# Layer 2 of a four-layer model: its fill between attention units handed out by a running credit, and tile pools that wait for the users of their own tile

## The chip, the core and the metric

The kernel runs on one core of one Trainium2 chip. A core has a matrix engine (TensorE, "PE" in the profile, with its weight loads shown apart as "PEld"), a vector engine (VectorE, "DVE"), a scalar engine (ScalarE, "ACT") that evaluates functions such as exp, tanh and gelu from tables, a general engine (GpSimd, "POOL") and a queue that issues most of the transfers (SyncE, "SP"). Matmul results land in PSUM, which this kernel splits into eight banks of 128 partitions by 512 fp32 numbers; everything else lies in SBUF. The engines run side by side and are held together by semaphores. The metric is the device time of one execution in microseconds.

## What is computed

The input `x` holds 8 sequences of 512 tokens with 128 features (fp32). Four layers follow one another, each of the same outer form: `xn = layernorm(x)`, then `x = x + attn(xn) * silu(ffn(xn))`. The layers differ in what attn and ffn are. Layer 0 is a recurrence with a routed ffn, layer 1 a feature-map attention with chosen experts, layer 3 a state-space block with an attention as its ffn. The change rewrites layer 2, which is this, for each sequence:

```python
def attn(x):                                   # 16 heads of 8 features
    q, k, v = split(ln(x, g_attn, b_attn) @ qkv_w + qkv_b)
    a = softmax(causal(q @ k.T / sqrt(8))) @ v  # for each head
    a = a @ out_w + out_b
    x = x + a
    ctx, xs, vs = a, ln(x, g1, b1), 0
    for _ in range(8):                          # ITERS
        u = tanh(ctx @ w_ctx + xs @ w_x + b_inl)
        vs = vs + 0.1 * (u - xs - vs)
        xs = xs + 0.1 * vs
    x = x + xs
    h = gelu(ln(x, g2, b2) @ ff_w1 + ff_b1)     # 512 wide
    return x + h @ ff_w2 + ff_b2

def ffn(x):                                     # hidden width 512
    h = silu(x @ w1.T * w1_s) * (x @ w2.T * w2_s)
    h = gelu(h @ h1.T * h1_s)
    h = gelu(h @ h2.T * h2_s)
    return h @ w3.T * w3_s
```

The product `ctx @ w_ctx` is the same in all eight iterations.

## The kernel before

The whole model is one program. Layers follow one another in time; `layer0`, `layer1`, `layer2` and `layer3` open their pools (SBUF tiles, and PSUM banks through `banks`, L95), load their packed constants (`load_consts`, L124, the load at L126 on SP's queue) and then issue their work. A tile pool puts tiles into memory that earlier tiles have left; the framework adds the waits for that. In layer 1 and 2, the order of PE is the order in which the code issues its matmuls (`manual_schedule`); the other engines' order follows from the same program text.

Between layers 1 and 2 stands `combine` (L176): it loads the experts' sum in two blocks (L184), takes its silu on ACT (L188), multiplies on DVE (L189) and adds to `x` on POOL (L194). Layer 2's first layernorm (L1226, with the subtraction at L1232) reads `x`. Between layers 2 and 3 the loads of layer 3's constants (L126 again) are the first thing that SP issues for layer 3, and its first matmul that needs them is L1658.

Layer 2 works with features on partitions. Its banks are `pu` (two tiles of two banks each, scores), `pf` (one bank, sums over keys) and `pa` (three banks, everything else).

- `begin(b)` (L1298): layernorm of sequence b, two transposes to feature order, projections to q, k and v (L1328 to L1345). The four heads of a group lie in strips of 32 partitions.
- `ffn(b)` (L1350): four steps of w1 and w2 with tanh for silu (L1359 to L1364), then h1 and h2. Each of these two is one step of sixteen 512-wide matmuls (L1372) with four gelus (L1373). Then one step of sixteen 128-wide matmuls for w3 (L1379).
- `maxima(b, g, qt)` (L1392): scores of query block qt against all keys up to it, 128 to 512 wide, four heads in two pairs. The matmuls at L1390 go to both `pu` tiles, a bf16 mask is added at L1401, and DVE takes the row maxima at L1404 into `mpad`. `put_maxima(b, g)` (L1406) transposes `mpad` (L1411) and adds it to a spare row of q (L1412), so that the scores come out with their maximum already taken off.
- `weights(b, g, kc)` (L1414): scores of key block kc against the queries from it on, 512 to 128 wide, again at L1390 into both `pu` tiles, with exp on ACT (L1422) and the causal cut on POOL.
- `sums(b, g, kc)` (L1426): weights times values and ones into `pf` (L1435), issued LAG = 2 units later.
- `group(b, g)` (L1443): transpose, divide by the sum, and for the last group of a sequence the output projection and `ctx` (L1466, L1468).
- `rest(b)` (L1471): layernorm, eight iterations (the matmuls L1485 with w_ctx and L1486 with w_x into one bank, tanh at L1488, updates on DVE at L1490 to L1493), layernorm, ff_w1 with gelu (L1509, L1510), ff_w2 in one step of thirty-two 128-wide records (L1515), and the gate and the addition to `x` (L1523 to L1527).

`begin`, `ffn`, `group` and `rest` are generators: each `yield` ends a step. One unit is one (sequence, group of four heads, key block), so a sequence has 16 units and the layer 128. The loop in `layer2` (L1531) issues for each unit u: its weights, one step of `back` (group and rest), at the end of a group the next `put_maxima`, one step of `front` (begin and ffn of the next sequence), the maxima of unit u + 5, one more step of back or front in turn, and the sums of unit u − 2. So each slot takes one step, however long that step is: between nothing and sixteen 512-wide matmuls. The five maxima ahead of the loop and all of `ffn(0)` come before the first weights; what is left of `rest` for the last two sequences comes after the last sums.

Of the kernel before, what the change touches and what calls it, by code (L numbers as in the profile page):

```python
# [80 lines left out]
class Kern:  # L81
# [12 lines left out]
    @contextmanager  # L94
    def banks(self, name, **bufs):  # L95

        with self.tc.tile_pool(name=name, bufs=1, space=PSUM) as pool:
            old, self.ps = self.ps, (pool, bufs)
            yield
            self.ps = old  # L100
# [230 lines left out]
def layer0(k, x, A, at):  # L331
# [5 lines left out]
    with ExitStack() as ctx:  # L337
        ctx.enter_context(k.banks("l0p", pa=5, pf=3))
        pool = lambda name, bufs=1, **kw: ctx.enter_context(tc.tile_pool(name=name, bufs=bufs, **kw))
# [123 lines left out]
        with tc.tile_pool(name="l0a", bufs=2) as tp, tc.tile_pool(name="l0a1", bufs=1) as tp1:  # L463
# [335 lines left out]
def choose1(k, cn, xT, idx, gate):  # L799
# [5 lines left out]
    with tc.tile_pool(name="ch", bufs=1) as pool, tc.tile_pool(name="ch2", bufs=2) as pool2:  # L805
# [112 lines left out]
class Layer1:  # L918
# [6 lines left out]
    def __init__(self, k, cp, x, A, at):  # L925
# [20 lines left out]
        with tc.tile_pool(name="l1a", bufs=2) as tp, tc.tile_pool(name="l1a1", bufs=1) as tp1:  # L946
# [16 lines left out]
    def choice_and_experts(self):  # L963
# [5 lines left out]
        with k.tc.tile_pool(name="l1w", bufs=2) as wp, k.tc.tile_pool(name="l1e", bufs=2) as ep:  # L969
# [163 lines left out]
def layer1(k, x, A, at):  # L1133
    nc, tc = k.nc, k.tc
    with ExitStack() as ctx:
        ctx.enter_context(k.banks("l1p", pu=2, pf=1, pa=3))
        pool = lambda name, bufs=1: ctx.enter_context(tc.tile_pool(name=name, bufs=bufs))
        L = Layer1(k, pool("l1c"), x, A, at)
        work = ExitStack()
        L.pools(lambda name, bufs: work.enter_context(tc.tile_pool(name=name, bufs=bufs)))  # L1140
# [40 lines left out]
def pack2(i):  # L1181
# [10 lines left out]
    p.add("own", one)  # L1192
    bq, bk = (strips2(b[None, n * C : (n + 1) * C]).reshape(2, P).T for n in range(2))
# [4 lines left out]
    bk[16::32] = -1.0  # L1198
    p.add("bk", bk)
# [58 lines left out]
class Layer2(BySequence):  # L1258


    def __init__(self, k, ctx, x, A, at):
        self.k, self.x = k, x
        nc, tc = k.nc, k.tc
        pool = lambda name, bufs=1: ctx.enter_context(tc.tile_pool(name="l2" + name, bufs=bufs))
# [33 lines left out]
    def begin(self, b):  # L1298

        k, nc, cn, tp = self.k, self.k.nc, self.cn, self.tp  # L1300
# [13 lines left out]
        yield  # L1314
        q["xT"] = tp.tile([P, T], F32, name="xT2", bufs=1)
        k.to_features(xn, q["xT"], nt=JT)
        yield
# [4 lines left out]
        yield  # L1322
        q["qT"] = tp.tile([P, 4, T], F32, name="qT2")
        q["kT"] = tp.tile([P, 2, T], F32, name="kT2")
        for t in range(2):
# [13 lines left out]
            yield  # L1339
# [8 lines left out]
        yield  # L1348

    def ffn(self, b):  # L1350
# [5 lines left out]
        for o in range(4):  # L1356
# [8 lines left out]
            yield  # L1365
        for n in ("h1", "h2"):
            src, hA = hA, hid()
            for o in range(4):
                ps = k.pa()
                for i in range(4):  # L1370
                    c0 = i * FF2 + o * P
                    nc.tensor.matmul(ps, fn[n][:, c0 : c0 + P], src[:, i, :], start=(i == 0), stop=(i == 3))  # L1372
                nc.scalar.activation(hA[:, o, :], ps, AF.Gelu, scale=fn[n + "_s"][:, o : o + 1])  # L1373
            yield
        f = q["f"] = tp.tile([P, JT, C], F32, name="f2", bufs=3)
        ps = k.pa((P, JT, C))
        for j in range(JT):
            for i in range(4):
                nc.tensor.matmul(  # L1379
                    ps[:, j, :], hA[:, i, j * P : (j + 1) * P], fn["w3"][:, i * C : (i + 1) * C],  # L1380
                    start=(i == 0), stop=(i == 3),
                )
# [779 lines left out]
```

## Time and profile before

Three runs of the kernel before took 3638.57, 3640.07 and 3646.86 us.

| | us |
|---|---|
| median of the runs | 3640.07 |
| the profiled execution, its own time | 3631.03 |
| its span (first to last instruction) | 3629.3 |
| layer 0 in the span | 0 to 885 |
| layer 1 | 885 to 1458 |
| layer 2 | 1458.6 to 2628.3 |
| of it: begin(0), five maxima, ffn(0) | 1458.6 to 1538.7 |
| of it: the 128 units | 1538.7 to 2558.0 |
| of it: the end of rest after the last sums | 2558.0 to 2628.3 |
| layer 3 | 2628.3 to 3629.3 |

Over the span PE is busy 2764.3 us (76%) with 16390 matmul instructions, DVE 2336.2 us (64%), ACT 1642.4 us (45%) and POOL 745.4 us (21%); the mean granted clock of PE is 0.835 of full speed. These are shares over stages with different limits, so each stage has to be read by itself. A row of the profile names a line of the code, an engine, an operation, its output and inputs with their shapes, how often it ran, and what the engine waited for just before it. Here is what a row of that kind looks like (from the page's part on the costliest groups: busy us, mean ns of one, idle us of the engine before it and what ended most of that):

```profile
L1372 PE MATMUL pa<-hid,f 128*128 128x512 f32 x512 | 222.7, 593 | 0.0
L1404 DVE TENSOR_REDUCE mpad<-pu 128x2 f32<-128x256 f32 (+3 forms) x256 | 199.2, 819 | 168.1 <-PE pu L1401 168.1
```

An fp32 matmul shows as two records in the trace, so L1372's 512 records are 256 matmuls. The mean of 593 ns is of the modelled durations, which overlap; the distance from one start to the next is what PE's time is made of. The row of granted clock over 40 slices, of which each is 90.7 us, reads 7 to 9 tenths in layer 2.

### The profile page before, as it was taken

Reading aid. Unit: us, or ns where it says so; the run is one execution under the profiler, and the core shown is the slowest. Engines: PE = TensorE matmul, PEld = TensorE weight load, DVE = VectorE, ACT = ScalarE, POOL = GpSimd, SP = SyncE. Lnnn points to the kernel's source line nnn. Section 1 sums busy time; section 2 is a strip of 40 time slices with the busy share of each in tenths; the row PEclk is TensorE's granted clock in tenths of the full one; section 3 lists DMA queues with packets and bytes.
Section 4 is the critical chain, followed back from the end, with each engine's and each line's share of the span. In section 5 each row is a group of like instructions: output and inputs, shape, how many; then the busy total and the mean of one; then the engine's idle time right before and its main releaser. Section 6 shows DMA issues by size and latency. Waiting matters only on the chain.

```text
span 3629.3 us, 44988 instructions
## 1 busy us (share of the span) xinstructions
PE 2764.3 (76%) x16390; PEld 1479.4 (41%) x16390; DVE 2336.2 (64%) x6346; ACT 1642.4 (45%) x3207; POOL 745.4 (21%) x845
## 2 busy tenths in 40 slices
PE   6164656512998898799999999998678877778777
PEld 4143444401444454344444444444334444444444
DVE  7989898998583234334445445445478787777776
ACT  5163545512544455233333333333266666655655
POOL 0004050400125553201101101101112222222121
PEclk8585757555789899799899899899878898878989
DMA  4003030311002222100000000000000000000000
GB/s 120 2 2 72 1 81 1 72 49 34 1 2 47 39 42 29 56 1 1 1 1 1 1 1 1 1 1 1 6 15 1 4 4 4 1 3 4 1 4 7
DMA packets 67519, 64.53 MB, mean 18 GB/s; under 512 B 5344, under 2 KB 59616, under 8 KB 66784
## 3 DMA queue, kind: packets, MB, share of 16 engines
q1 hardware_dynamic: 39264, 42.75, 3.8%
q0 software_dynamic: 19712, 14.69, 3.1%
q10 hardware_dynamic: 8320, 4.19, 0.4%
q8 instruction: 129, 2.11, 0.2%
q14 instruction: 94, 0.77, 0.1%
HBM read 43.80 MB, written 17.83 MB: 17 GB/s over the span
## 4 chain that ended last, share of the span: by engine, by line
PE 35%; DVE 16%; ACT 7%; issue 2%; POOL 2%; DMA 0%; POOLq 0%; ACTq 0%; DVEq 0%; SPq 0%
PE pa L1372 6%; PE pu L1390 6%; DVE nm L1972 4%; ACT at L1973 3%; PE pu L1969 3%; PE pf L1954 2%; DVE mpad L1404 2%; PE pf L1435 2%; PE pa L1486 1%; PE pa L1485 1%; ACT at L1422 1%; PE pa L1878 1%; PE pa L1509 1%; PE pa L1359 1%; PE pa L1515 1%
## 5 line engine op out<-in xcount | busy, mean ns | idle before, releaser
L1973 ACT ACTIVATE at<-pu,nm 128x512 f32<-128x512 f32 x512 | 347.9, 688 | 174.3 <-DVE nm L1972 154.5
L1972 DVE TENSOR_REDUCE nm<-pu 128x1 f32<-128x512 f32 x512 | 327.4, 683 | 75.4 <-PE pu L1969 74.8
L199 POOL TENSOR_SCALAR_AFFINE_SELECT at<-at 128x512 f32<-128x512 f32 x184 | 123.6, 672 | 1000.2 <-ACT at L1422 851.7
L1404 DVE TENSOR_REDUCE mpad<-pu 128x2 f32<-128x256 f32 (+3 forms) x256 | 199.2, 819 | 168.1 <-PE pu L1401 168.1
L1422 ACT ACTIVATE at<-pu 128x1024 f32<-128x1024 f32 (+3 forms) x256 | 171.8, 702 | 283.5 <-PE pu L1390 283.2
L1078 ACT ACTIVATE at<-pu,rsqrt 128x1024 f32<-128x1024 f32 (+3 forms) x256 | 191.1, 793 | 191.0 <-PE pu L1073 161.2
L1372 PE MATMUL pa<-hid,f 128*128 128x512 f32 x512 | 222.7, 593 | 0.0
L1969 PE MATMUL pu<-qT,kT 32*128 32x512 f32 x1024 | 203.1, 731 | 2.4 <-ACT at L1973 2.3
L1390 PE MATMUL pu<-qT,kT 32*128 32x512 f32 (+3 forms) x1024 | 160.6, 514 | 56.4 <-DVE mpad L1404 41.8
L748 PE MATMUL pa<-ident,Y 128*128 128x128 f32 x32 | 7.9, 425 | 211.2 <-DVE Y L739 211.2
L1954 PE MATMUL pf<-at,va 128*32 128x512 f32 x1024 | 163.1, 715 | 0.4 <-POOL va L1947 0.4
L1390 PE MATMUL pu<-kT,qT 32*128 32x128 f32 (+3 forms) x1024 | 150.8, 565 | 14.7 <-ACT at L1422 10.5
L548 POOL DMA_INDIRECT xg<-xn_d,idx x48 | 55.1, 1147 | 499.5 <-PE pf L552 318.5
L1372 PEld LDWEIGHTS pa<-hid,f 128*128 128x128 f32 x512 | 96.6, 190 | 119.5 <-issue 118.9
L1493 DVE SCALAR_TENSOR_TENSOR X<-X,u 128x512 f32<-128x512 f32 x56 | 38.7, 691 | 156.7 <-ACT u L1488 156.7
L1073 PE MATMUL pu<-qT,kT 32*128 32x512 f32 (+3 forms) x1024 | 130.3, 513 | 4.9 <-ACT at L1078 3.9
L1016 POOL DMA_INDIRECT f_d<-ys,idx x64 | 105.0, 1640 | 140.0 <-DMA f_d<-ys,idx 85.2
L1947 POOL TENSOR_TENSOR va<-V,sm 128x32 f32<-128x32 f32 x128 | 36.7, 286 | 463.6 <-DVE sm L1946 384.0
L1390 PEld LDWEIGHTS pu<-qT,kT 32*128 32x128 f32 x1024 | 67.3, 196 | 154.4 <-DVE mpad L1404 114.3
L1373 ACT ACTIVATE hid<-pa,f 128x512 f32<-128x512 f32 x64 | 44.0, 688 | 172.5 <-PE pa L1372 172.5
L1083 DVE TENSOR_TENSOR at<-at,ceiling 128x512 f32<-128x512 f32 x72 | 50.0, 695 | 102.3 <-ACT at L1078 91.4
L700 DVE TENSOR_TENSOR Z<-Hs,KE 128x96 f32<-128x96 f32 x510 | 108.8, 253 | 0.9
(610 smaller groups left out, 6682.8 us busy)
## 6 DMA issues: line engine op xcount, KB each, us to landing
w<-in_w_dram SPq DMA_DIRECT2D x24, 512.0 KB, 3.7
f_d<-zeros ACTq DMA_DIRECT2D x8, 512.0 KB
xn_d<-xn SPq DMA_DIRECT2D x8, 512.0 KB, 5.0
w<-in_w_dram SPq DMA_DIRECT2D x16, 256.0 KB, 3.2
w<-in_w_dram SPq DMA_DIRECT2D x24, 128.0 KB
f<-in_f_dram SPq DMA_DIRECT2D x1, 2888.0 KB, 11.9
xn<-in_x_dram SPq DMA_DIRECT2D x4, 512.0 KB, 9.0
Gt<-in_x_dram SPq DMA_DIRECT2D x4, 512.0 KB
```

What stands on the lines that cost most here:

```text
L199: self.nc.gpsimd.affine_select(a, a if src is None else src, pattern, ALU.is_ge, 0.0, base=0, channel_multiplier=-1)
L700: nc.vector.tensor_tensor(z[:, 0:3, v, :], bc(prev[:, v, :], 1, 3), bc(KE[:, o + t, 0:3, :], 2, 4), ALU.mult)
L1073: nc.tensor.matmul(pu[:, n, 0:m], q["kT"][r, g // 2, kc * P : kc * P + P], q["qT"][r, g, kc * P :], start=True, stop=True,)
L1078: nc.scalar.activation(at_[:, i : i + 2, 0:m], pu[:, :, 0:m], AF.Square, bias=k.rsqrt2, scale=32.0**-0.5)
L1372: nc.tensor.matmul(ps, fn[n][:, c0 : c0 + P], src[:, i, :], start=(i == 0), stop=(i == 3))
L1390: self.k.nc.tensor.matmul(pu[:, n, 0:m], a[r, c0 : c0 + P], b[r, q0 : q0 + m], start=True, stop=stop)
L1404: nc.vector.tensor_reduce(top[:, i : i + 2, 16], pu[:, :, 0:m], AX.X, ALU.max)
L1422: nc.scalar.activation(at_[:, i : i + 2, 0:m], pu[:, :, 0:m], AF.Exp, scale=8.0**-0.5)
L1954: nc.tensor.matmul(po[i * 32 : i * 32 + 32, :], va[:, kc, c0 : c0 + 32], E[:, i, :], start=(kc == 0), stop=(kc == JT - 1))
L1969: nc.tensor.matmul(pu, q["kT"][r, kc * P : (kc + 1) * P], q["qT"][r, g, :], start=True, stop=True)
L1972: nc.vector.tensor_reduce(nm[:, w], pu, AX.X, ALU.max, negate=True)
L1973: nc.scalar.activation(E[:, n, :], pu, AF.Exp, bias=nm[:, w], accum_out=sm[:, w])
```

## The change

The change has two parts.

**Pools.** Every tile pool and every group of banks in all four layers is opened with `reuse_waits="tile"`: a new tile waits for the users of the tiles whose bytes it takes, and not for users of the old pool as a whole. Nothing else changes in layers 0, 1 and 3.

```diff
-        with self.tc.tile_pool(name=name, bufs=1, space=PSUM) as pool:
+        with self.tc.tile_pool(name=name, bufs=1, reuse_waits="tile", space=PSUM) as pool:
```

The same argument is added in layer 0 (its main pools and "l0a"), in the choice of experts ("ch", "ch2"), in layer 1 ("l1a", "l1w", "l1e" and its main and work pools), and in the pools of layers 2 and 3.

**Layer 2's order.** Steps now yield what they cost in passes of a 512-wide matmul, and the loop hands them out by a running credit. The long steps are cut: h1 and h2 into half-steps of two matmuls, w3 and ff_w2 into halves, ff_w1 into two. The gelus of h1 and h2 read a bank of their own (`ph`), for which `pa` gives one up.

```diff
-        ctx.enter_context(k.banks("l2p", pu=2, pf=1, pa=3))
+        ctx.enter_context(k.banks("l2p", pu=2, pf=1, pa=2, ph=1))
...
             for o in range(4):
-                ps = k.pa()
+                ps = k.psum("ph", (P, T))
                 for i in range(4):
+                    if i == 2:
+                        yield 2.0
                     c0 = i * FF2 + o * P
                     nc.tensor.matmul(ps, fn[n][:, c0 : c0 + P], src[:, i, :], start=(i == 0), stop=(i == 3))
                 nc.scalar.activation(hA[:, o, :], ps, AF.Gelu, scale=fn[n + "_s"][:, o : o + 1])
-            yield
+                yield 2.0
```

`w_ctx @ ctx` is computed once for a sequence, at the end of `group`, and copied to SBUF; each iteration of `rest` adds it on DVE:

```diff
+        ps = k.pa()
+        nc.tensor.matmul(ps, cn["w_ctx"], ctx, start=True, stop=True)
+        q["ctx"] = tp.tile([P, T], F32, name="cw2")
+        nc.scalar.copy(q["ctx"], ps)
+        yield 1.0
...
-            nc.tensor.matmul(ps, cn["w_ctx"], q["ctx"], start=True, stop=False)
-            nc.tensor.matmul(ps, cn["w_x"], now, start=False, stop=True)
+            nc.tensor.matmul(ps, cn["w_x"], now, start=True, stop=True)
             u = tp.tile([P, T], F32, name="u2")
-            nc.scalar.activation(u, ps, AF.Tanh, bias=cn["b_inl"], scale=0.01)
+            nc.vector.tensor_tensor(u, ps, q["ctx"], ALU.add)
+            nc.scalar.activation(u, u, AF.Tanh, bias=cn["b_inl"], scale=0.01)
```

The maxima of two groups go to two spare rows of one `mpad` and are put into q together, so the maxima run nine units ahead (AHEAD = PAIR + 1) and not five, and their order inside a group is turned by one, which sets the wide weights beside narrow maxima:

```diff
+            top = self.mpad[g // 2][:, qt, :].rearrange("p (i c) -> p i c", c=32)
+            nc.vector.tensor_reduce(top[:, i : i + 2, 16 + g % 2], pu[:, :, 0:m], AX.X, ALU.max)
+
+    def put_maxima(self, b, t):
+
+        k, nc, qT, put = self.k, self.k.nc, self.q[b]["qT"], self.cn["put"]
         ps = k.pa((P, JT, P))
+        for qt in range(JT):
+            nc.tensor.transpose(ps[:, qt, :], self.mpad[t][:, qt, :], k.ident)
+        top = ps.rearrange("p a b -> p (a b)")
+        for v in range(2):
+            to = qT[:, 2 * t + v, :]
+            nc.vector.scalar_tensor_tensor(to, top, put[:, v : v + 1], to, ALU.mult, ALU.add)
```

And the loop: two slots in each unit, one behind the weights and one behind the maxima. A slot takes at most one step of group or rest, and then steps of begin and ffn of the next sequence (`front`) as long as its credit lasts.

```diff
+        U = 4 * JT
+        PAIR = 2 * JT
+        AHEAD = PAIR + 1
+        def maxima(u):
+
+            b, g, n = units[u]
+            L.maxima(b, g, (n - 1) % JT)
+
+        first = L.ffn(0)
         for u in range(AHEAD):
+            maxima(u)
+            next(first, None)
...
+        def fill(u, second):
+
+
+            nonlocal credit
+            wide = 1.5 - u % JT
+            share = (2.4 + 0.6 * wide, 2.4 - 0.6 * wide)[second] if u >= U else 1.8
+            share += 0.3 - 0.6 * second
+            passes = next(groups, None)
+            if passes is None:
+                passes = 0.0 if second and u % 2 == 0 else next(rest, 0.0)
+            credit = min(credit, share) + share - passes
+            while credit > 0.0:
+                passes = next(front, None)
+                if passes is None:
+                    break
+                credit -= passes
+
         for u in range(len(units) + LAG):
             b, n = divmod(u, U)
             if u < len(units):
                 held[u] = L.weights(*units[u])
+                if u % PAIR == PAIR - 1 and u + 1 < len(units):
+                    L.put_maxima(units[u + 1][0], units[u + 1][1] // 2)
+            fill(u, False)
             if u + AHEAD < len(units):
+                maxima(u + AHEAD)
+            fill(u, True)
             if u >= LAG:
                 wb, g, kc = units[u - LAG]
                 L.sums(wb, g, kc, held.pop(u - LAG))
                 if kc == JT - 1:
+                    groups = chain(groups, L.group(wb, g))
                     if g == 3:
+                        rest = chain(rest, L.rest(wb))
+
+            if n == LAG - 1 and b + 1 < B:
+                front = chain(L.begin(b + 1), front, L.ffn(b + 1))
+        for _ in chain(groups, rest):
+            next(front, None)
```

The lines that this block takes the place of are the loop described above (L1531 on). `w3` and `ff_w2` follow the same pattern as h1 and h2, two blocks of 128 tokens at a time, each half with its own PSUM tile and its own DVE instruction.

## The prediction

> **What bounds the kernel.** I read the busy rows by stretch first, because shares over the span mix four layers. Columns: window, its length, busy us (and instructions) of PE, PE's weight loads, DVE, ACT, POOL, then granted PE clock, DMA share, GB/s. The rows are layer 2's body (first weights to last of them), its steady part, two neighbouring pieces of one sequence, one piece split by clock, and the tail.
>
> ```profile
> 1538.70:2558.00 1019.30, 950.16 (x5335) 443.59 (x5334) 468.70 (x743) 366.85 (x529) 130.34 (x170) 0.93 0.00 1
> 1708.00:2399.30 691.30, 648.93 (x3572) 306.75 (x3571) 326.50 (x526) 251.46 (x362) 91.55 (x115) 0.93 0.00 1
> 2039.00:2083.00 44.00, 38.49 (x241) 19.56 (x244) 22.82 (x42) 15.79 (x22) 10.95 (x12) 0.77 0.00 1
> 2083.00:2122.60 39.60, 38.11 (x230) 16.86 (x223) 26.61 (x42) 16.80 (x26) 4.17 (x6) 1.00 0.00 1
> 2069.70:2083.40 13.70, 12.08 (x60) 5.90 (x60) 7.04 (x14) 3.21 (x5) 4.53 (x5) 0.50 0.00 0
> 2558.00:2628.30 70.30, 46.73 (x170) 23.93 (x170) 24.81 (x41) 15.49 (x23) 6.68 (x7) 0.81 0.00 0
> ```
>
> In the body DVE works 46% and ACT 36%; PE is the bound at 93% busy. Equal counts (241 and 230) take 44.0 and 39.6 us, though the first piece holds the narrower matmuls; it is at clock 0.77. PE's timeline (start, length, instruction, count, idle before) shows why:
>
> ```profile
> 1984.20 13.90 PE L1372 MATMUL pa<-hid,f 128*128 128x512 f32 x32
> ...
> 2060.81 1.14 PE L1390 MATMUL pu<-qT,kT 32*128 32x512 f32 x8
> 2061.88 3.84 PE L1515 MATMUL pa<-c,hid 128*128 128x128 f32 x32
> 2065.65 0.71 PE L1390 MATMUL pu<-kT,qT 32*128 32x256 f32 x8
> ...
> 2068.56 1.72 PE L1390 MATMUL pu<-qT,kT 32*128 32x384 f32 x8 [1.29 <-DVE mpad L1404]
> 2070.44 2.39 PE L1390 MATMUL pu<-kT,qT 32*128 32x384 f32 x8 [0.17 <-ACT at L1422]
> ```
>
> A whole h-step (13.9 us of PE) goes between two units, and then there is none for tens of us, in which PE waits for the score banks `pu`: for the maxima on DVE or the exp on ACT. The waits of layer 2 give the sum (us, times, longest):
>
> ```profile
> PE pu L1390 <- DVE mpad L1404: 45.7, 73, 1.7
> PE pu L1390 <- ACT at L1422: 23.5, 46, 1.5
> ```
>
> So 69 us are plain stall. The slowed matmuls add more: 512-wide strip groups take 1.07 us there (2060.81 to 2061.88) and 2.1 us at half clock.
>
> **PE's floor.** Pitches at full clock from these starts: a 512-wide fp32 record 0.43 us ((1998.03−1984.20)/32; one matmul is two records, 0.86); a 128-wide one 0.118 (3.77/32); strip groups of eight 1.07/0.86/0.65/0.43 by width; sums 0.99/0.79/0.59/0.36; a mask group 0.23. Per sequence: 130 wide records 55.9, 136 narrow ones 16.0, weights 4×3.01=12.0, maxima 12.0, masks 16×0.23=3.7, sums 4×2.73=10.9: 110.5 us against a period of 138.3 (the first h-step of each sequence starts at 1846.4, 1984.4, 2122.9). Summed over the body's records: 802 of 1019.3 us, a ratio of 1.27. The packed pieces do better: 2083–2122.6 floor 33.8 (1.17), 1950–1984 29.7 (1.144), 2016–2039 20.2 (1.14), all at clock 1.00; 2039–2083 25.3 (1.74).
>
> **The evening (fill, half-steps, order of maxima).** It moves no work off PE; it spreads a sequence's 66 us of fill (begin, ffn, group, rest) over 32 slots, about 2 us (2.4 passes of 0.86 from the second sequence on) behind every weights and every maxima. A score bank then has a slot plus a narrow neighbour to come free: a pair's maxima take DVE 0.42 to 1.22, its exp 0.39 to 1.02 on ACT. I take 1.14, the ratio of the two packed pieces that mix all kinds. The ends: 1.10 (single-group starts, no switching cost left) and 1.27 (nothing evened).
>
> **Removed from PE.** Per sequence 7 of 8 w_ctx matmuls (7×0.86=6.0), over seven sequences in the body 42; put_maxima once for two groups: 16×4 transposes less, 7.6; four maxima moved to the prologue, 2.4. New body floor 802−52=750. ×1.14=855: **−164**, of which 52×1.27=66 would come without evening.
>
> **Added.** DVE: one 0.69 us add per recurrence iteration, 5.5 a sequence, 65 to 71 us of 116: hidden beside fill. Each iteration is one slot, and its chain (matmul 0.86, add, tanh, update at 0.69) takes 3.2 us of some 3.6 between slots; uncovered it is 56×0.69=39. ACT: the gelus of h1 and h2 now stand alone between exps, so table loads rise from 29 to 133 by the built order; L1373's go from 8 to 55 and L1422's from 14 to 66. Shown before:
>
> ```profile
> L1422 ACT ACT_TABLE_LOAD x14 | 18.0, 1283 | 12.7 <-PE pu L1390 12.7
> L1373 ACT ACT_TABLE_LOAD x8 | 10.3, 1283 | 0.1
> ...
> 2062.03 1.28 ACT L1422 ACT_TABLE_LOAD   x1 [1.21 <-PE pu L1390]
> 2063.33 1.94 ACT L1422 ACTIVATE at<-pu 128x1024 f32<-128x1024 f32 x2
> ```
>
> 104×1.283=133 us more on ACT: 50 to 68 us per sequence of 116 (58%), and an exp whose load comes first frees its banks 1.28 late. The Trainium skill, "ScalarE: Activation LUTs", § What ACT_TABLE_LOAD costs, adds 1.38 us of drain to each, 2.66 in all, and its advice to batch calls by table set speaks against this change. By it ACT gets 277 us, 86 us per sequence of 116, and loads would reach PE. Here the exp starts 0.02 us after its load ended, so no drain: I take 133 us, and put its part on PE at nothing beyond the 1.14 (bounds 0 and 133). The single `ph` bank keeps a next step out until its gelu is done (load 1.28+0.69+0.25); the other half-step comes a slot later, so 0 (bounds 0 and 64×0.7=45).
>
> A second rule: "TensorE: Matmul & The Clock Gate", § HAM oscillation, asks for no PE-idle gaps above about 3.4 us. The idle pieces here are 1.5 us at most, so by it the evening could not bring the clock back. Half clock fills about 20 us of each 138 (6.8 and 13.7 us around 2046 and 2070), worth 10 us a sequence, 75 in all: the body would gain 89, the median be 3551. The trace halves the clock just where these small gaps cluster, in each sequence, so I keep the 164.
>
> **Prologue** (begin(0), maxima, ffn(0), 80 us): nine maxima interleaved with ffn instead of five ahead; stalls go, `ph` adds a gelu wait: 0±5. **Tail:** rest(7) alone, its iteration is
>
> ```profile
> 2592.11 0.69 ACT L1488 ACTIVATE u<-pa,c 128x512 f32<-128x512 f32 x1 [1.94 <-PE pa L1486]
> 2592.83 0.69 DVE L1493 SCALAR_TENSOR_TENSOR X<-X,u 128x512 f32<-128x512 f32 x1 [1.14 <-ACT u L1488]
> 2593.58 1.12 PE L1486 MATMUL pa<-X,c 128*128 128x512 f32 x2 [0.65 <-DVE X L1493]
> ```
>
> 2.63 us, with w_ctx's matmul hidden beside ACT. The add stands on this chain: 8×(0.69+0.04)=+6; halves of ff_w2 give 1 back: **+5**.
>
> **Pool waits.** Instruction order in layers 0, 1 and 3 is the same. Layer 1 to 2:
>
> ```profile
> 1442.93 7.70 SPq L184 DMA_DIRECT2D cmb_f<-f_d  x4
> ...
> 1449.32 2.36 DVE L189 TENSOR_TENSOR cmb_sg<-cmb_sg,s 128x1024 f32<-128x1024 f32 x2 [2.27 <-ACT cmb_sg L188]
> 1463.06 1.29 DVE L1232 TENSOR_TENSOR xn<-x,s 128x512 f32<-128x512 f32 x2 [2.23 <-POOL x L194]
> ```
>
> The loads waited for a DVE multiply at 1442.5; now only for the last scatter (issued 1431.5). SP carries them alone then, so Silu no longer ends the wait: 2.3 us. L1232 waits for its own tile, not POOL's last add: **−5** (0 to −7). Layer 2 to 3:
>
> ```profile
> 2636.12 0.56 PE L1658 MATMUL pa<-meet,c 128*128 128x4 f32 x2 [7.88 <-DVE meet L1655]
> ```
>
> Layer 3's constants still wait for layer 2's last ff_w2 matmul, so both loads queued on SP come as late: 0. Layer 0 to 1: the first gather moves 1 us earlier beside a bound DVE: 0.
>
> **Sum:** −164−5+5+0=−164. Profiled 3631.03→3467; the median of the runs is 9.04 higher, so **3476**.
>
> **Rivals.**
> A, evened as worked, ratio 1.11–1.19: 832–893 us of body, own range 3453–3515. Chance 0.60.
> B, the stalls nearly vanish (1.10 and below): 825, 3446 and down to 3425. For it: nothing but DVE and ACT latency stood behind them. Against: no mixed piece is that tight. 0.11.
> C, banks still come late (a unit's slot can be four transposes, 0.5 us, and two `pa` banks replace three) and only the removed work counts: 1.20–1.27, 3519–3574. 0.13.
> D, slower: table loads on PE's path. Place: exp at L1422 behind a gelu; `weights` and `maxima` share two `pu` pairs, so a load ahead of exp holds PE. Price: 104×1.28=133 less the 66 of removed work: +67, 3707 (3851 with the page's drain). It decides when evening brings nothing and each load costs PE over 66/104=0.64 us; had evening its full worth, 164/104=1.58 would be needed, more than a load lasts. For it: stalls on exp are there already. Against: after a load of before PE had a filled slot. 0.14.
> E, it does not do what it says: pool waits are unmoved where SP's next load hangs on the last matmul, and order gains nothing: about 3640. 0.02.
>
> **Numbers.** 3476 is A's. The range 3430–3580 holds A, C and half of B; D and the rest of B are out. A measurement tells about 0.2% (7 us; the runs spread over 8) from no change: faster A+B+C less a sliver 0.83, same 0.03, slower 0.14.
>
> **What would show it.** Body near 855 us and 116 us per sequence; clock near 1.00 throughout it; L1390's two waits mostly gone; 133 loads of 1283 ns with no PE wait behind them; tail iterations of 3.36 us; L1232 at about 1458. Wrong if PE's waits on L1422 or on L1373 (`ph`) grow past 60 us, or the clock stays at 0.93.

## The result and the profile after

Nine runs of the changed kernel have a median of 3628.42 us (3620.68 to 3629.41), nine of the kernel before, made beside them, 3640.07 (3634.27 to 3646.86). The ratio is 0.9964 with a 95% interval of 0.9954 to 0.9974: 9 to 17 us faster, where 164 were forecast. The profiled execution has a span of 3627.4 us, 1.9 us less than that of the kernel before, whose profiled execution lies 9 us under its median. So the rows below tell where time moved, and the runs tell how much it came to.

The rows by stretch come first again. The body now begins where the first ffn ends and ends at the last sums matmul, points that every kernel below has (the prediction's body, 1538.7 to 2558.0, was cut a little differently). The first two rows are of the kernel before, body and tail:

```profile
1535.50:2574.20 1038.70, 964.72 (x5421) 451.91 (x5419) 473.07 (x749) 371.54 (x535) 132.62 (x172) 0.93 0.00 1
2574.20:2628.80 54.60, 34.43 (x114) 16.80 (x102) 22.23 (x37) 10.81 (x16) 4.75 (x5) 0.81 0.00 0
```

and these are of the changed kernel:

```profile
1534.80:2553.50 1018.70, 899.25 (x5204) 401.12 (x5205) 505.00 (x810) 504.92 (x646) 131.97 (x172) 0.94 0.00 1
2553.50:2619.60 66.10, 33.32 (x100) 13.82 (x92) 27.54 (x45) 11.53 (x17) 5.67 (x6) 0.64 0.00 0
```

PE is busy for 65 us less in the body, but the body is only 20 us shorter: PE's idle (length less busy) went up from 74 to 119 us, and its clock is 0.94 where a packed piece has 1.00. The pitch floor of the body's records fell from 813.7 to 758.8 us, so the ratio to the floor rose from 1.28 to 1.34. (The floor is the prediction's: for each matmul record its distance to the next at full clock.) The tail is 11.5 us longer, at clock 0.64 in place of 0.81. ACT's busy time in the body rose by 133 us.

The two long waits of PE in the body of the kernel before (us, times, longest), with 8 us of others beside them:

```profile
PE pu L1390 <- DVE mpad L1404: 41.8, 68, 1.7
PE pu L1390 <- ACT at L1422: 23.5, 46, 1.5
```

and the longest of the changed kernel's, 118 us in all:

```profile
PE pu L1404 <- ACT at L1440: 29.5, 36, 1.9
PE pu L1404 <- DVE mpad L1419: 20.2, 19, 3.0
PE pa L1337 <- DVE xa L172: 12.8, 4, 5.4
PE pa L1507 <- DVE X L1515: 9.4, 10, 2.8
PE ph L1385 <- ACT hid L1386: 7.6, 7, 1.8
PE pa L1467 <- ACT oT L120: 6.1, 10, 1.5
PE pa L1370 <- DVE u L1509: 6.1, 5, 1.7
PE pa L168 <- DVE hr L1240: 6.0, 4, 4.1
```

The wait for maxima on DVE is halved, which is what the evening was to do. The wait for exp is 6 us longer. And the rows below these two hardly existed before. Most are waits for the inputs of the fill itself: `xa`, X, oT, the layernorm's `hr`, 43 us with the shorter rows of that kind. The row of L1370 is another kind. L1370 is w2's matmul, which does not read `u`; it waits until the add at L1509 has read the `pa` bank that it writes to. With six shorter rows of things that the waiting matmul does not read, PE waits 17.6 us for one of the two `pa` banks. Before, with three banks, no row of this kind is in the body.

The loads in front of exp stand in this group of the page (busy us, mean ns of one, idle before and what ended it):

```profile
L1440 ACT ACT_TABLE_LOAD x66 | 84.7, 1283 | 89.8 <-PE pu L1404 88.8
```

There are 133 table loads in layer 2, as forecast, of 1283 ns. The last column is the one that matters: ACT was idle for 88.8 us before these 66, and what ended the idle time was PE's scores. So the load mostly does not start when the gelu is done and ACT has nothing to do; in 47 of the 66 cases it starts after ACT has waited for the scores. (18 follow directly on other work of ACT.) The timeline of the changed kernel shows one of the 47, and what it holds up on PE:

```profile
2057.26 0.71 PE L1404 MATMUL pu<-qT,kT 32*128 32x256 f32 x8
2058.05 1.28 ACT L1440 ACT_TABLE_LOAD   x1 [3.11 <-PE pu L1404]
2058.14 0.66 PE L1467 MATMUL pa<-ident,oT 128*128 128x128 f32 x4 [0.17 <-DVE oT L122]
...
2059.34 1.09 ACT L1440 ACTIVATE at<-pu 128x512 f32<-128x512 f32 x2
2059.99 2.14 PE L1404 MATMUL pu<-kT,qT 32*128 32x384 f32 x8 [1.19 <-ACT at L1440]
```

ACT had been idle for 3.11 us when the scores came at 2058.05. Exp could have started there; the load comes first, and exp starts at 2059.34, 0.01 us after its end. PE does the one short fill step of that slot and then stands idle for 1.19 us, nearly as long as the load.

### The profile page after: what moved, and what is told of

It is laid out like the page before. It is cut to its first block, busy times and chain, and to the rows that moved or that the text cites. A ratio compares the mean times of both kernels' runs of the same rounds, so it can differ in the third digit from the quotient of the medians.

```text
span 3627.4 us, 44779 instructions
## 1 busy us (share of the span) xinstructions
PE 2698.3 (74%) x16214; PEld 1423.2 (39%) x16214; DVE 2384.1 (66%) x6426; ACT 1776.3 (49%) x3319; POOL 744.9 (21%) x845
## 3 DMA queue, kind: packets, MB, share of 16 engines
q8 instruction: 127, 2.08, 0.2%
## 4 chain that ended last, share of the span: by engine, by line
PE 31%; DVE 15%; ACT 10%; issue 2%; POOL 1%; POOLq 0%; ACTq 0%; DVEq 0%
PE pu L1404 5%; PE ph L1385 5%; DVE nm L2025 4%; ACT at L2026 3%; PE pu L2022 3%; PE pf L2007 2%; PE pf L1453 2%; ACT at L1440 2%; ACT L1440 1%; PE pa L1507 1%; DVE mpad L1419 1%; PE pa L1931 1%; PE pu L1416 1%; PE pa L1910 1%; POOL rs L1755 1%
## 5 line engine op out<-in xcount | busy, mean ns | idle before, releaser
L1419 DVE TENSOR_REDUCE mpad<-pu 128x2 f32<-128x1024 f32 (+3 forms) x256 | 198.9, 818 | 149.8 <-PE pu L1416 149.7
L1385 PE MATMUL ph<-hid,f 128*128 128x512 f32 x512 | 255.6, 626 | 11.6 <-ACT hid L1386 11.5
L1404 PE MATMUL pu<-kT,qT 32*128 32x512 f32 (+3 forms) x1024 | 135.7, 502 | 30.3 <-ACT at L1440 29.5
L1404 PE MATMUL pu<-qT,kT 32*128 32x512 f32 (+3 forms) x1024 | 127.2, 493 | 20.7 <-DVE mpad L1419 20.2
L1385 PEld LDWEIGHTS ph<-hid,f 128*128 128x128 f32 x512 | 94.6, 199 | 113.8 <-issue 89.7
L1073 PE MATMUL pu<-qT,kT 32*128 32x512 f32 (+3 forms) x1024 | 131.0, 515 | 4.8 <-ACT at L1078 4.0
L1016 POOL DMA_INDIRECT f_d<-ys,idx x64 | 104.6, 1635 | 138.2 <-DMA f_d<-ys,idx 86.8
L1440 ACT ACT_TABLE_LOAD x66 | 84.7, 1283 | 89.8 <-PE pu L1404 88.8
L585 POOL DMA_INDIRECT f_d<-ys,idx x48 | 83.9, 1748 | 109.9 <-ACT ys L584 81.2
L1404 PEld LDWEIGHTS pu<-kT,qT 32*128 32x128 f32 x1024 | 56.9, 189 | 123.3 <-ACT at L1440 79.6
```

What stands on the lines that cost most here:

```text
L1073: nc.tensor.matmul(pu[:, n, 0:m], q["kT"][r, g // 2, kc * P : kc * P + P], q["qT"][r, g, kc * P :], start=True, stop=True,)
L1404: self.k.nc.tensor.matmul(pu[:, n, 0:m], a[r, c0 : c0 + P], b[r, q0 : q0 + m], start=True, stop=stop)
L1419: nc.vector.tensor_reduce(top[:, i : i + 2, 16 + g % 2], pu[:, :, 0:m], AX.X, ALU.max)
L1440: nc.scalar.activation(at_[:, i : i + 2, 0:m], pu[:, :, 0:m], AF.Exp, scale=8.0**-0.5)
```

## The experiments

Each was run beside the kernel before; the ratio is to it. Names that begin with b are edits of the kernel before, those with a of the changed kernel. The table puts layer 2's body side by side (us; idle is length less PE busy; all from one profile each).

| kernel | body | PE busy | idle | PEclk | tail | ratio of times, interval |
|---|---|---|---|---|---|---|
| before | 1038.7 | 964.7 | 74 | 0.93 | 54.6 | 1 |
| b_hoist | 1053.0 | 929.2 | 124 | 0.93 | 68.0 | 1.0068 [1.0046, 1.0090] |
| changed | 1018.7 | 899.3 | 119 | 0.94 | 66.1 | 0.9964 [0.9954, 0.9974] |
| a_nohoist | 1053.0 | 933.2 | 120 | 0.94 | 55.1 | 1.0020 [1.0003, 1.0037] |
| a_tanh | 948.0 | 862.9 | 85 | 0.96 | 67.8 | 0.9778 [0.9757, 0.9800] |
| a_tanh_nohoist | 983.8 | 902.6 | 81 | 0.95 | 54.0 | 0.9844 [0.9825, 0.9862] |
| a_tanh_loose | 925.7 | 857.5 | 68 | 0.97 | 50.4 | 0.9662 [0.9635, 0.9690] |
| a_pre | 994.7 | 884.7 | 110 | 0.95 | 69.3 | 0.9906 [0.9886, 0.9927] |

**The loads taken away: a_tanh.** It computes tanh where the layer has gelu, and so needs no second table.

```diff
-                nc.scalar.activation(hA[:, o, :], ps, AF.Gelu, scale=fn[n + "_s"][:, o : o + 1])
+                nc.scalar.activation(hA[:, o, :], ps, AF.Tanh, scale=fn[n + "_s"][:, o : o + 1])
...
-            nc.scalar.activation(hid[:, o, :], ps, AF.Gelu, bias=cn["ff_b1"][:, o : o + 1])
+            nc.scalar.activation(hid[:, o, :], ps, AF.Tanh, bias=cn["ff_b1"][:, o : o + 1])
```

> The changed kernel with layer 2's gelus (h1, h2 and ff_w1) computed as tanh, so that exp and all of layer 2's functions come from one table and its 133 table loads fall away; instructions, shapes and order otherwise the same. Theory L (the extra table loads, 133 us of ACT, delay exp, gelu and tanh, and PE waits for them): PE's 118 us of idle in the body fall below 50, and the time goes from 3628 to about 3500 (3470 to 3540). Rival S (steps of the fill that depend on one another stand only one slot apart, and the latency of DVE and ACT without any load is already longer than a slot): the idle stays above 90 us, the time above 3595.

Measured: 0.9778, 3551.8 us. Against the changed kernel's 0.9964 that is 1.9% or 68 us, and its body is 71 us shorter. Over the 104 added loads that is 0.65 us each (0.68 by the body; the 29 old ones cost nothing, as the next run shows). PE's order is the same; its idle fell by 34 us and its busy time by 36, as the clock rose from 0.94 to 0.96. In the body of a_tanh the two kinds of wait on score banks read

```profile
PE pu L1404 <- DVE mpad L1419: 18.9, 20, 3.0
...
PE pu L1404 <- ACT at L1440: 2.8, 4, 1.1
```

so the wait for exp was made of loads (29.5 to 2.8 us), and the wait for maxima was not. Theory L holds for this part, but 85 us of idle are no matter of loads, and both the idle and the time lie between the two theories. Of the waits left, 21.7 us are for score banks, 17.9 for `pa` banks and 42 for inputs of the fill.

**The same in the order before: b_tanh.** The same two lines in the kernel before.

> The kernel before with the same three gelus as tanh: 29 table loads (37 us of ACT) fall away. Theory L: they stand mostly behind whole h-steps with ACT idle, so at most 20 us: 3620 to 3640. Rival S: 3635 to 3640. It is also the base for the run with tanh of the changed kernel: the gain of the new order without loads is the difference of the two.

Measured: 1.0012 [1.0005, 1.0019]: nothing gained. The 29 loads of the old order cost nothing. The likely reason is that PE had a long step beside them, as the ff_w2 step of 3.84 us beside the load at 2062.03 in the prediction's lines. (In both tanh kernels the order of a few DVE and ACT instructions in layer 3 shifts as well; its length there, 1012 and 1006 us, lies within the 1000 to 1012 that it has in all the profiles.)

**The pools alone: b_pools.** The `reuse_waits` argument on every pool and bank of the kernel before, no other edit.

> The kernel before with the pools' argument alone (every tile pool and bank waits by tile). Theory P1: it brings only the earlier combine between layers 1 and 2, 3 to 5 us: 3635 to 3637. Rival P2: it makes the whole measured difference of 12 us, and the new order of layer 2 brings nothing: 3626 to 3630.

Measured: 1.0005 [0.9996, 1.0015], no difference. Its profile shows the table load of layer 2's first exp at 1526.1 us where it was 1533.0, so the earlier entry is there; the body behind it was 9 us longer in that execution (clock 0.92). P2 is out: the 12 us are not the pools'. That the entry's gain reaches the end is not shown.

**w_ctx: a_nohoist, b_hoist, a_tanh_nohoist.** The first and the last put the matmul back into each iteration of the changed kernel, b_hoist takes it out of the kernel before (there with plain `yield`s). Each of these edits also takes away or adds the step of `group` in which the single matmul stands:

```diff
-            nc.tensor.matmul(ps, cn["w_x"], now, start=True, stop=True)
+            nc.tensor.matmul(ps, cn["w_ctx"], q["ctx"], start=True, stop=False)
+            nc.tensor.matmul(ps, cn["w_x"], now, start=False, stop=True)
             u = tp.tile([P, T], F32, name="u2")
-            nc.vector.tensor_tensor(u, ps, q["ctx"], ALU.add)
-            nc.scalar.activation(u, u, AF.Tanh, bias=cn["b_inl"], scale=0.01)
+            nc.scalar.activation(u, ps, AF.Tanh, bias=cn["b_inl"], scale=0.01)
```

> The changed kernel with w_ctx put back into each iteration (two matmuls, tanh straight from PSUM, no add on DVE). Theory H1 (PE's time is what counts, so the 42 us of matmuls taken off come back whole, times 1.1): 3660 to 3675, the tail 6 us shorter. Rival H2 (the chain of an iteration is what PE waits for, and the add on DVE made it 0.73 us longer 64 times): 3615 to 3640.

> The kernel before with w_ctx computed once in a sequence and added on DVE, nothing else: 56 matmuls of 0.86 us less, 49 us of PE. H1 (PE's time counts): 35 to 60 us faster. H2 (the longer chain takes a part back, as in the new order, where it was worth 20 to 24): 15 to 25 us faster, the tail 6 longer.

> The changed kernel with layer 2's gelus as tanh (no loads) and w_ctx back in each iteration: the evened order without loads and without the removed matmuls. Against the same kernel with w_ctx once, H1 (PE's time counts): 42 us and more slower, about 3597 where that took 3552. H2 (the longer chain of an iteration takes the gain back): within 20 us of it. Against the kernel before with tanh (3635) it gives what evening alone is worth: by the prediction's ratio 1.14 some 100 us, by what the runs have shown so far 30 to 50.

Measured: in the changed order the single w_ctx is worth 0.56% (1.0020 to 0.9964, 20 us), without loads 0.66% (24 us): 34 to 36 us in the body less 11 to 14 in the tail, between H1 and H2. But this is not w_ctx alone. Without its step, all of `rest` comes one slot earlier, and one slot in four takes no step of `rest`. In the changed kernel such a slot lies between the second layernorm of `rest` and the transposes that read it; in a_nohoist and a_tanh_nohoist the two are in neighbouring slots. (The kernel before has an empty step behind each layernorm of `rest`, which the new order drops.) PE's wait for `hr`, 6.0 us in the changed kernel and 7.4 in a_tanh, is in these two

```profile
PE pa L168 <- DVE hr L1240: 35.9, 7, 6.2
PE pa L168 <- DVE hr L1240: 33.4, 7, 5.0
```

so 30 and 26 us of the 34 and 36 may belong to where a step fell, and not to the matmul. No run separates them.

In the old order the single w_ctx costs 0.7%, 25 us (14 in the body, 13 in the tail), which neither theory had. PE is busy for 35 us less in the body and idle for 50 more. PE's waits in b_hoist's body:

```profile
PE pu L1390 <- DVE mpad L1404: 59.8, 65, 4.0
PE pu L1390 <- ACT at L1422: 19.2, 36, 1.5
PE pa L1490 <- DVE X L1498: 13.2, 15, 1.9
PE pa L1503 <- DVE X L1498: 9.0, 7, 2.6
PE pa L1514 <- ACT hid L1515: 7.9, 6, 1.3
```

The wait for the maxima is 18 us longer, and of the last three rows only the first was there before, with 0.5 us. A reading that fits, but was not tried by itself: DVE has 56 more adds in its queue, and where an iteration is the only fill of a slot, half its matmul time covers half as much.

From a_tanh_nohoist against b_tanh (0.9844 to 1.0012) the evened order with the pools is worth 1.7%, 61 us, with w_ctx in place and no loads (30 to 50 were expected), and this in spite of the 33.4 us of waiting for `hr`. With loads it is worth nothing: a_nohoist is 7 us slower than the kernel before. Step by step the measured change is +4 us from the kernel before to b_tanh, −61 to a_tanh_nohoist, +64 for the loads to a_nohoist and −20 to the changed kernel: −13. How the −61 and the −20 divide between the order and w_ctx stays open because of the wait for `hr`.

**The place of the load: a_pre, a_pre_m, a_m.** A one-column exp behind the gelus draws the load to where ACT is free:

```diff
                 nc.scalar.activation(hA[:, o, :], ps, AF.Gelu, scale=fn[n + "_s"][:, o : o + 1])
-                yield 2.0
+                b and nc.scalar.activation(self.warm, hA[:, o, 0:1], AF.Exp, scale=0.0); yield 2.0
```

and the same behind each pair of ff_w1's gelus. The scheduler still orders ACT by itself and puts the small exp behind a waiting one in a fourth of the cases, so a_pre_m holds ACT to program order; a_m does only that.

> The changed kernel with a one-column exp behind every gelu of layer 2 (not in the first ffn), and ACT held in program order there: there are 13 table loads more than in the changed kernel (146), but the load back to exp's table starts as soon as the gelu is done, not when the next scores have arrived on PE. Theory L1 (what hurts is the load's place, between the arrival of the scores and exp): PE's waits on exp fall from 29 us to under 10, the time by 30 to 60 us. Rival L2 (what hurts is the sum of the loads on ACT, wherever they stand): no gain, or slower by up to 15 us.

> The changed kernel with ACT held in program order in layer 2 and nothing else: the control for the run with the early load. All theories: within 10 us of the changed kernel, about 0.996 of the kernel before.

> The changed kernel with a one-column exp behind every gelu of layer 2 (not in the first ffn), ACT's order left to the scheduler as in the changed kernel: 146 loads, of which 54 of the 73 back to exp start with the gelu's end. Theory L1 (place of the load): with ACT held in order the same edit brought 0.7%; here 15 to 30 us faster than the changed kernel, 0.988 to 0.992 of the kernel before. Rival L2 (sum of the loads): 13 loads more, 0 to 10 us slower, 0.997 to 0.999.

Measured: a_pre_m 1.0011 [1.0000, 1.0022] against a_m 1.0080 [1.0063, 1.0096], 25 us faster with 13 loads more, a little under L1's 30 to 60. PE's wait for exp fell from 34.0 to 12.2 us, but that for oT, which ACT copies, rose from 9.2 to 27.7. a_m as a control missed: program order on ACT alone is 1.2% slower than the changed kernel, with 28.6 us of waiting for begin's layernorm that are not there in the changed kernel. a_pre is 0.9906, 21 us faster than the changed kernel. Its loads:

```profile
L1386 ACT ACT_TABLE_LOAD x57 | 73.1, 1283 | 1.0
L1387 ACT ACT_TABLE_LOAD x39 | 50.0, 1283 | 0.7
L1440 ACT ACT_TABLE_LOAD x19 | 24.4, 1283 | 9.7 <-PE pu L1404 9.2
```

L1387 is the small exp. These 39 loads back to exp's table start with hardly any idle before them (0.7 us in all), and only 19 loads still stand in front of an exp of scores. PE's wait for exp fell from 29.5 to 18.0 us. ACT's sum of loads went up by 17 us and the time down by 21: the load's place counts (L1), though not for all of the 68.

**Fewer loads: a_pair_m, a_g4, a_g4_gap.** a_pair_m gives `ph` two banks and `pa` one, and issues two gelus together. a_g4 scales on DVE and has one gelu for all four hidden blocks; a_g4_gap also lets the next slot go without a front step:

```diff
-                nc.scalar.activation(hA[:, o, :], ps, AF.Gelu, scale=fn[n + "_s"][:, o : o + 1])
-                yield 2.0
+                nc.vector.tensor_scalar(hA[:, o, :], ps, fn[n + "_s"][:, o : o + 1], None, ALU.mult)
+                if o == 3:
+                    nc.scalar.activation(hA, hA, AF.Gelu)
+                yield 2.0 if o < 3 else 4.4
```

(a_g4 has a plain `yield 2.0` there.)

> The changed kernel with two `ph` banks and one `pa`, the gelus of h1 and h2 in pairs, ACT in program order in layer 2: 83 loads and not 133. Theory L2 (sum of the loads): 50 loads of 1.28 us less, up to 38 us faster by the share that all 133 cost (66 of 170 us). Theory L1: as many exps with a load ahead as there are gelu pairs, 25 fewer, 15 to 30 us faster. Rival: the lone `pa` bank costs more than that, no gain or slower.

> The changed kernel with h1's and h2's scale applied on DVE (0.69 us each, which frees the `ph` bank), and one gelu over all four hidden blocks when the last is there: 57 table loads and not 133. Theory L (loads): 76 of the 104 added loads go, worth some 50 us by what all were worth (68): 0.982 to 0.987 of the kernel before. Rival S (dependent steps too close): h2's first matmul and w3's now wait for a gelu of 2 us and its load, some 4 us twice in a sequence, 60 us in all: no gain, 0.995 to 1.005.

> The same, and the step with the gelu counts 2.4 passes more, so that the next slot takes no front step, while each slot's share is 0.15 higher. Theory S: the wait for the gelu is covered by the units' own work, 15 to 40 us faster than without the gap. Theory L alone: the same within 8 us.

Measured: a_pair_m 1.0261 [1.0238, 1.0283], 66 us slower than its control a_m: the lone `pa` bank costs far more than 50 loads bring. (Wq's matmul alone waits 17.6 us there until kT's copy has read the bank, 2.3 in the control.) a_g4 0.9950 [0.9937, 0.9963], the same as the changed kernel although 76 loads are gone; rival S. With the gap 0.9904 [0.9883, 0.9925], 17 us faster than without, as S said. In a_g4 the wait for exp is 10 us shorter than in the changed kernel, but h2's and w3's matmuls wait 16.6 us for the single gelu. With the gap these 16.6 us are gone; the wait for `xa` fell as well (12.8 to 1.9) and that for exp rose (19.8 to 27.9), since the gap moves every later step of the fill. So distance behind a gelu helps, but the 17 us are not its own alone.

**The fill's own chains: a_tanh_loose.** On a_tanh, two dependences taken away by other data:

```diff
-            nc.tensor.matmul(ps, cn["w_x"], now, start=True, stop=True)
+            nc.tensor.matmul(ps, cn["w_x"], q["xT0"], start=True, stop=True)
...
-            nc.tensor.matmul(ps, cn["Wk"][:, ts], xa, start=True, stop=True)
+            nc.tensor.matmul(ps, cn["Wk"][:, ts], q["xT"], start=True, stop=True)
```

> The changed kernel without loads (gelus of layer 2 as tanh), and with two dependences of the fill taken away by other data: w_x's matmul of each iteration reads the ctx product and not the newest X, and the projections to q and k read xT, which is a step older than xa. Same matmuls, same shapes. Theory S (the fill's own chains are the idle that is left, and keep the clock down): PE's idle in the body falls from 85 to some 55 us, the time by 25 to 45 us, to 0.966 to 0.971 of the kernel before. Rival R (the idle moves to the next wait, the score banks): idle above 70 us, less than 15 us gained, 0.974 to 0.978.

Measured: 0.9662, 42 us below a_tanh, of which the tail is 17 (an iteration is no chain there any more). The body is 22 us shorter with 17 us less idle, from 85 to 68. The two waits that were taken away had been 24 us in a_tanh, so a part moved on to other waits. S has the direction and the size of the time, partly by the tail; the idle lies between both. Wk's and Wq's wait shows how such a chain becomes late. DVE in the changed kernel, and PE behind it:

```profile
2071.80 0.69 DVE L1240 TENSOR_TENSOR hr<-hr,rs 128x512 f32<-128x512 f32 x1 [1.20 <-POOL rs L1246]
2072.41 2.35 DVE L1419 TENSOR_REDUCE mpad<-pu 128x2 f32<-128x1024 f32 x2
2074.68 0.80 DVE L172 TENSOR_SCALAR xa<-pa,c 128x512 f32<-128x512 f32 x1
2075.62 2.05 PE L1337 MATMUL pa<-xa,c 128*128 128x512 f32 x2 [5.43 <-DVE xa L172]
```

PE had finished the transposes for `xa` at 2070.2. The copy stands in DVE's queue behind a layernorm of `rest` that waits for POOL, and behind a pair of the widest maxima, until 2074.68; PE, which had finished the step before, waits for 5.43 us.

**Together: best1, best2.** a_g4_gap with the small exp behind the gelus; best2 also copies `xa` on ACT.

> The changed kernel with one gelu over four hidden blocks, the gap behind it, and a one-column exp behind it and behind each pair of ff_w1's gelus: 64 loads, most of those back to exp right behind their gelu. Theory L1 and S together: the two edits add up in part, 0.982 to 0.988 of the kernel before. Rival: both took the same loads away, 0.989 to 0.991.

> The same, with begin's xa copied out of PSUM on ACT and not on DVE, where it stood behind rest's layernorm and a pair of maxima (5.4 us of PE's time where it was worst, 13 in all). Theory S: 5 to 12 us faster than without this. Rival (ACT is as late there): within 4 us.

Measured: 0.9905 [0.9873, 0.9937] and 0.9898 [0.9864, 0.9932]: no better than a_pre or a_g4_gap alone within the intervals; the rivals' numbers. But the rival's reason, the same loads taken away twice, is not all of it. In best1 only 11 loads in front of exp are left (28 in a_g4_gap), with 1 us of idle before them and not 29, and PE's wait for exp is still 26.1 us (27.9). One of these waits shows what holds exp now:

```profile
1946.97 1.91 ACT L1389 ACTIVATE hid<-hid 128x2048 f32<-128x2048 f32 x1 [2.61 <-DVE hid L1387]
...
1948.90 1.28 ACT L1444 ACT_TABLE_LOAD   x1
...
1951.06 2.01 PE L1408 MATMUL pu<-kT,qT 32*128 32x256 f32 x8 [2.90 <-ACT at L1444]
```

Exp and its load stand on ACT behind the gelu over four blocks, which itself waits for its last input. These four (a_pre, a_g4_gap, best1, best2) are faster than both kernels of this study, by 1.0% and 0.6%.

## Why the prediction was wrong

**The step that failed** is the ratio in the body's term: "I take 1.14, the ratio of the two packed pieces that mix all kinds", applied to the new floor, 750×1.14=855. In the points used here the new floor is 758.8 us and 1.14 of it 865; the body took 1018.7, a ratio of 1.343. Without loads it would be 1.249 (948.0), without loads and two chains 1.220 (925.7). The packed pieces do not mix all kinds. The two h-steps of that sequence lie at 1984.2 to 1998.0 and 1998.9 to 2012.8, between the pieces, and its ff_w1 at 2056.5. So none of the three packed pieces holds a gelu, and none a table load. Their fill is short steps like these:

```profile
1967.51 1.02 PE L1359 MATMUL pa<-xT,f 128*128 128x512 f32 x2
1968.37 1.02 PE L1360 MATMUL pa<-xT,f 128*128 128x512 f32 x2
1969.32 1.14 PE L1390 MATMUL pu<-kT,qT 32*128 32x512 f32 x8
...
1973.49 0.50 PE L1390 MATMUL pu<-qT,kT 32*128 32x128 f32 x8
1973.92 1.12 PE L1485 MATMUL pa<-ctx,c 128*128 128x512 f32 x2
1974.89 1.02 PE L1486 MATMUL pa<-X,c 128*128 128x512 f32 x2
```

They are already even, about 1.9 us of fill in a slot, and three of these four matmuls read something that has been there for slots (`xT`, `ctx`). What the evening newly spread between the units was the other kind: h1, h2 and ff_w1 with their gelus; and it did so with one bank fewer in `pa` and without the layernorms' empty steps. The forecast took a ratio from the fill that has no gelu and applied it to all of it.

**The table loads** are the term inside it that was mis-sized. I counted 133 of them, 1283 ns each, and 133 us on ACT, all of it right, and then put "its part on PE at nothing beyond the 1.14 (bounds 0 and 133)". It measured 68 us (a_tanh; 64 with w_ctx in the iterations). The argument for nothing was ACT's share, 58% of the period; measured 50% of the body. A share does not tell when the load runs: the row for L1422's loads that I quoted had 12.7 us of idle that ended with PE's scores, for 14 loads, and I read only the duration in it. Rival D had this mechanism and its place (exp behind a gelu, both `pu` pairs held), with a limit of 0.64 us for each load if the evening brought nothing; each costs 0.65 to 0.68. D's other half was wrong: the evening does bring 61 us.

**The rivals.** Without loads the kernel stands at 0.9778 of the kernel before, which is 3559 of its 3640 us, inside rival C's range (3519 to 3574), and C's reason is there too: `pa` banks and inputs of the fill come late. The changed kernel can be read as C with D's loads on top, between the two. E's 3640 is the nearest number, but its reason, that order gains nothing, is refuted: the order's 61 us and the 64 us of loads cancel. That the change came out faster at all, as forecast, is for the same reason more luck than insight. Of the two signs named for being wrong, the waits for exp and `ph` stayed under 60 us (29.5 and 7.6), and the clock, at 0.94, hardly left 0.93.

**The drain**: the Trainium skill, "ScalarE: Activation LUTs", § What ACT_TABLE_LOAD costs, would have made a load 2.66 us. In the changed kernel too exp starts 0.01 us behind the load, so the row was the right choice. The page's advice to batch by table set pointed the right way, but a_g4, which batches, gained nothing until the next step stood further off.

**The clock**: the Trainium skill, "TensorE: Matmul & The Clock Gate", § HAM oscillation, warns of idle gaps above about 3.4 us. In the body before, PE's waits were 1.7 us at most, but for one of 3.1 (I wrote 1.5), and the clock was still 0.50 from 2069.7 to 2083.4. I expected near 1.00 once the gaps had gone. It is 0.94 after, 0.96 without loads, 0.97 with looser chains. Within the new order it rose as the idle fell; but the kernel before had 0.93 with only 74 us of idle, so the sum of the idle does not set it. PE's busy time stayed at 1.19 of the floor (964.7 of 813.7, 899.3 of 758.8), so this part of the ratio did not move at all, and the other part, the idle, grew.

**Removed work**: 42 us of w_ctx matmuls in the body. PE is busy for 34 us less than in a_nohoist (40 without loads), and the body is 34 us shorter (36), but with the wait for `hr` in it. How much of the 42 came back is not shown.

**Tail**: +5 forecast, +11.5 measured. The add and its 0.73 us are there, but an iteration takes 4.4 us and not 3.36:

```profile
2574.00 0.69 DVE L1515 SCALAR_TENSOR_TENSOR X<-X,u 128x512 f32<-128x512 f32 x1 [0.79 <-ACT u L1510]
2574.73 0.69 DVE L1514 SCALAR_TENSOR_TENSOR X<-X,X 128x512 f32<-128x512 f32 x1
...
2574.75 2.08 PE L1507 MATMUL pa<-X,c 128*128 128x512 f32 x2 [2.26 <-DVE X L1515]
2576.86 0.69 DVE L1509 TENSOR_TENSOR u<-pa,cw 128x512 f32<-128x512 f32 x1 [1.44 <-PE pa L1507]
```

The matmul runs for 2.08 us where it took 1.12: 8×0.96=7.7 us, beside 5.8 for the adds. In the kernel before, w_ctx's matmul of the next iteration ran in the pause; it cost nothing, and with it PE was busy for 2.1 of each 2.63 us at a clock of 0.81 over the tail. The experiments repeat it: with w_ctx in the iteration the tail has clock 0.84 to 0.85 and 54 to 55 us (a_nohoist, a_tanh_nohoist), without it 0.60 to 0.63 and 68 to 69 us (b_hoist, a_tanh, a_pre). I called it hidden; it very likely also kept the clock, though the add that lengthens the pause came with each removal.

**Prologue** 0±5: 79.0 us from layer 2's first instruction to its first weights before (1458.57 to 1537.56), 79.9 after (1455.58 to 1535.48). **Layer 1 to 2** −5: the subtraction at L1232 started at 1463.06, now

```profile
1457.92 3.39 DVE L1238 TENSOR_TENSOR xn<-x,s 128x512 f32<-128x512 f32 x2
```

5.1 us earlier, but the pair takes 3.39 us beside POOL's addition where it took 1.29. The first weights come 2.1 us earlier than before. **Layer 2 to 3** and **layer 0 to 1**: nothing, as forecast. Layer 3 took 7 us longer in this profile than in that of before, with the same order; over all profiles it takes 1000 to 1012 us with no tie to an edit that I found, and this stays open.

What also stays open: 83 of the 154 us by which the body misses 865 are no matter of loads. 22 of them go with the two chains that were loosened. The wait for maxima (19 us), the two `pa` banks (18 us), the missing empty steps behind the layernorms and the rest of the fill's waits were seen and not tried one by one.

## What to carry to other kernels

When work is spread evenly to cover waits, count what the spreading splits: each function of another table between two of the first costs a load, and the load is paid where its instruction waits, not where the engine is free. Before a ratio from a dense stretch is applied to a new order, list what that stretch leaves out; here it left out every gelu. A step whose input was made a slot ago needs cover itself, and in an experiment that moves a step by one slot, look for what else that slot was covering. A matmul in a pause of a dependent chain may be worth keeping for the clock even where its result could be had for less.

## What the runs showed of the chip

The table load in front of exp began when the scores arrived, in 47 of 66 cases after ACT had stood idle; a one-column exp behind the gelu drew it forward and brought 21 to 25 us for 13 loads more. With eight hidden matmuls taken out of a chain of eight iterations, and an add put in, PE's clock in the tail was 0.64 and not 0.81, and an iteration took 4.4 us and not 2.63, of which the added instruction is 0.73. On ACT, a gelu that waited 2.61 us for its input held up the exp behind it, and so PE for 2.90 us.
